# Operand stage of a state-space layer: silu's half folded into weights, its bias as matrix products, evictions and a normalisation on other engines

## The chip, the cores and the metric

The kernel runs on one core of one Trainium2 chip. The metric is the device time of one execution in microseconds. Five engines have instruction queues of their own, each worked through in order: TensorE (PE in the profile; its weight loads are PEld), VectorE (DVE), ScalarE (ACT), GpSimd (POOL), and SyncE (SP), which here only issues transfers. An instruction that waits holds up everything behind it in its own queue, and nothing in the others.

## The reference, cut to what matters

Four residual layers are applied to `x` of 4 images x 128 channels x 64 x 64 pixels, each of the form `x = x + layer(group_norm(x))`: self-attention over the 4096 pixels, a 5x5 convolution, a selective state-space scan in both directions, and a 3x3 convolution. The change lies in the third layer's inputs:

```python
t = einsum('oc,bchw->bohw', Wx, x) + bx          # x is the group-normed image
xc = sum(conv_w[:, k] * up[:, :, k:k+L] for k in range(4))   # causal, 4 taps over t
xc = silu(xc + conv_b)
delta = softplus(xt @ Wd + bd)                   # xt is xc transposed
Bm = xt @ WB
Cm = xt @ WC
# scan: h = exp(delta * A) * h + (delta * xt) * Bm ; y = sum over states of h * Cm + D * xt
```

The two directions have weights of their own for 64 channels each, so that they fill the 128 partitions together. silu is made from a tanh: `silu(p) = (tanh(p/2) + 1) * p/2`.

## The kernel before, in words

The last layer needs nothing from other images, so the images are pipelined. A generator `images()` produces the work of all images in order: attention, the 5x5 convolution (`conv_pairs`), then `scan_prep` and `scan_operands`, which make the scan's operands and store them in DRAM. A second generator, `scan_core`, produces the scan: 256 ticks per image. The main loop writes the program out by hand: after each half tick it takes as much of `images()` as a credit allows (`PACE` 2.8 units per tick, 1.5 for the last image), and each piece of work yields its cost in these units. So attention and convolution of image b+1 stand beside the scan of image b, and the order of every engine's queue is fixed when the program is built. Waits come from the data and from the buffers.

**A tick** of the scan (128 rows x 1024 positions) is: `drive`, a product db on GpSimd (L1027); `decay`, two exponentials da on ScalarE (L1020); `recur`, two scans on VectorE (L1037), which are either followed by two products with the row of C on VectorE (L1040), or by one on GpSimd (`weigh`, L1058); and `collect`, products y on TensorE (L1072) that sum over states. The rows of B and C are read back from DRAM. ScalarE keeps the last column of each scan (L1053).

**The operand stage** (`scan_operands`) works on eight pieces of 512 positions, in slots of an explicit schedule. A slot costs 0.7 units, and a new piece begins every five slots. The steps of piece i, with the slot after its start:

- slots 0 and 1: `taps`, 16 instructions on TensorE (L832): four taps, two directions in two column halves, two instructions each, into the single PSUM bank pt (tag `s`). For the first piece products with `edge` (L838) correct the border.
- slot 4: `halves` on ScalarE: L846 writes (pt + bias)/2 to xc in SBUF, L851 writes tanh((pt + bias)/2), for images 1 to 3 in place over pt, for image 0 to a buffer `w` in SBUF.
- slot 5: `silu` on VectorE (L855): (th + 1) * xc into xc. Only then is the bank pt free for the next taps (for image 0 after L851).
- slots 8, 9 and 12: products with the block-diagonal weights `bdiag` on TensorE (L864), m=0 for delta, m=1 for B, m=2 for C. The products for B and C share one bank (tag `a`).
- slots 11 and 13: `row` on ScalarE (L869) copies B (m=1) and C (m=2) from PSUM to a buffer `w` of four, which SyncE stores.
- slots 10, 12 and 13: `softplus` (L877, L878), `exp` (L904, L909) on ScalarE, `digits` on VectorE (L883, L884).
- after half of the pieces `logs` (L913) on ScalarE, then `join` (L889) and `drives` (L894) on GpSimd.

In one slot, what belongs to an earlier piece stands ahead of what belongs to a later one, and `digits` ahead of `row` for C.

Interleaved with the slots of image b is the start of image b+1: its load, its statistics on VectorE (L378), its group norm, four pieces of `normalise` on ScalarE in place (L369, 1024 columns each), and eight products `keys` pv on TensorE (L396) with copies by ScalarE (L401). After these, attention begins with the scores sc (L464).

Of the kernel before, what the change touches and what calls it, by code (L numbers as in the profile page):

```python
# [24 lines left out]
F32 = mybir.dt.float32  # L25
I32 = mybir.dt.int32
AF = mybir.ActivationFunctionType
ALU = mybir.AluOpType
# [4 lines left out]
P = 128  # L33
# [3 lines left out]
MM = 512  # L37
HALF = P // 2
# [10 lines left out]
BQ, BK, BX, BP, CONVB, BD, DSKIP, MAINB, CONVW, ALOG = 0, 1, 2, 3, 4, 5, 6, 7, 8, 12  # L49
# [3 lines left out]
def conv_preact_kernel(  # L53
# [16 lines left out]
    nc = tc.nc  # L70
# [12 lines left out]
    scale = float(C) ** -0.5  # L83
# [3 lines left out]
    const = ctx.enter_context(tc.tile_pool(name="const", bufs=1))  # L87
# [3 lines left out]
    pools, ready = {}, set()  # L91

    def bank(tag, name):
        return pools.get(tag, ps).tile([P, MM], F32, tag=tag, name=name)
# [20 lines left out]
    ident = const.tile([P, P], F32, name="ident")  # L115
# [11 lines left out]
    def col(i):  # L127
        return vec[:, i : i + 1]


    ssm_sb = early.tile([P, 3, HALF], F32, name="ssm_sb")
    nc.scalar.dma_start(ssm_sb, ssm)
    bdiag = const.tile([P, 3, C], F32, name="bdiag")
    nc.gpsimd.memset(bdiag, 0.0)
    for d in range(2):
        r = slice(d * HALF, (d + 1) * HALF)
        nc.gpsimd.tensor_copy(bdiag[r, :, r], ssm_sb[r, :, :])


    NK, NQ = P // SG, NST // NI  # L140
# [10 lines left out]
    skip = const.tile([P, P], F32, name="skip")  # L151
# [25 lines left out]
    wtap = const.tile([P, KC, C], F32, name="wtap")  # L177
    edge = const.tile([P, KC - 1], F32, name="edge")
    cbias = small.tile([P, 1], F32, tag="cbias", bufs=1, name="cbias")
    hbias = const.tile([P, 1], F32, name="hbias")  # L180

    def scan_constants():

        for k in range(KC):
            ptap = bank("z", f"ptap{k}")[:, :C]
            nc.tensor.matmul(
                ptap, col(CONVW + k).to_broadcast([P, P]), ident, start=True, stop=True
            )
            yield HOP
            nc.vector.tensor_tensor(wtap[:, k, :], wm[:, 3, :], ptap, ALU.mult)  # L190
        for t in range(KC - 1):

            nc.vector.tensor_reduce(
                edge[:, t : t + 1], vec[:, CONVW : CONVW + KC - 1 - t], AX.X, ALU.add
            )
        nc.vector.tensor_tensor(cbias, edge[:, 0:1], col(CONVW + KC - 1), ALU.add)
        nc.vector.scalar_tensor_tensor(cbias, cbias, col(BX), col(CONVB), ALU.mult, ALU.add)
        nc.vector.tensor_scalar(edge, edge, col(BX), -1.0, ALU.mult, ALU.mult)
        nc.vector.tensor_scalar(hbias, cbias, 0.5, None, ALU.mult)
        yield HOP  # L200
        mine = early.tile([P, NI], F32, name="mine")
        nc.vector.tensor_reduce(
            mine, ident.rearrange("p (s i) -> p i s", i=NI), AX.X, ALU.add
        )
        rates = every.rearrange("p k q i -> p (k q) i")
        mine = mine.unsqueeze(1).to_broadcast([P, NK * NQ, NI])
        nc.vector.tensor_tensor(rates, rates, mine, ALU.mult)
        nc.vector.tensor_reduce(a_neg, rates, AX.X, ALU.add)
        yield HOP
        nc.scalar.activation(a_neg, a_neg, AF.Exp)  # L210
        nc.vector.tensor_reduce(
            sel, ident.rearrange("p (s i) -> p s i", i=NI), AX.X, ALU.add
        )
        nc.vector.tensor_scalar(skip, ident, col(DSKIP), None, ALU.mult)
        yield HOP
        nc.vector.tensor_scalar(a_neg, a_neg, -1.0, None, ALU.mult)
        yield HOP
# [66 lines left out]
    def large(n, name):  # L284
        return pools["big"].tile([P, ASIZE], F32, tag=f"A{n % 2}", name=name)
# [6 lines left out]
    def stats_tile(name):  # L292
        return small.tile([P, NM, 6], F32, tag=f"gn_st{name[0]}", name=f"st_{name}")
# [74 lines left out]
    def normalise(dst, src, gn):  # L368
        nc.scalar.activation(dst, src, AF.Identity, scale=gn[0], bias=gn[1])  # L369
# [4 lines left out]
    def attention_start(b, xn):  # L374

        st = stats_tile(f"a{b}")
        for i in range(NM):
            nc.vector.bn_stats(st[:, i, :], xn[:, bass.ts(i, MM)])  # L378
            yield 0.0
        gn = yield from group_norm(st, f"a{b}")  # L380
        while b > 0 and (b - 1, "taps") not in ready:
            yield 0.0
        v = pools["big"].tile([P, VSIZE], F32, tag="V", name=f"v_{b}")
        v = v[:, : NJT * C].rearrange("p (j c) -> p j c", c=C)
        pvs = {}

        def piece(i):
            cut = bass.ts(i, L // 4)
            normalise(xn[:, cut], xn[:, cut], gn)

        def keys(i):

            tag = "s" if b > 0 else "saz"[i % 3]
            pvs[i] = bank(tag, f"pv_{b}_{i}").rearrange("p (t c) -> p t c", c=C)
            for t in range(TPM):
                nc.tensor.matmul(  # L396
                    pvs[i][:, t, :], xn[:, bass.ts(i * TPM + t, P)], wv, start=True, stop=True
                )

        def take(i):  # L400
            nc.scalar.copy(v[:, i * TPM : (i + 1) * TPM, :], pvs.pop(i))  # L401

        piece(0)
        yield SLOT
        for i in range(NM):
            if i % 2 == 0 and i // 2 + 1 < 4:
                piece(i // 2 + 1)
            keys(i)
            yield SLOT
            if b > 0:  # L410
                take(i)
                yield 0.0
            elif i > 0:
                take(i - 1)
        if b == 0:
            take(NM - 1)
        return xn, v
# [394 lines left out]
    def scan_operands(b, xn, mats4, piece):  # L812
# [5 lines left out]
        xc = large(b, f"xc_{b}")[:, :L]  # L818
        delta = pools["big"].tile([P, L], F32, tag="xt", name=f"delta_{b}")
        pts, ths, pzs, pbs, us = {}, {}, {}, {}, {}  # L820

        def taps(i, *ks):
# [4 lines left out]
            for k in ks:  # L827
                lo = L + 2 * pad - 1 - k - t - (MM - 1)
                views = (xn[:, t + k : t + k + MM], xn[:, lo : lo + MM][:, ::-1])
                for d, view in enumerate(views):  # L830
# [6 lines left out]
                    if i == 0 and k == 0:  # L837
# [2 lines left out]
                            tile_position=(0, d * HALF), skip_group_check=True,  # L840
                        )

        def halves(i):

            pt = pts.pop(i)
            nc.scalar.activation(xc[:, bass.ts(i, MM)], pt, AF.Identity, scale=0.5, bias=hbias)  # L846

            ths[i] = pt if b > 0 else pools["bg"].tile(
                [P, MM], F32, tag="w", bufs=4, name=f"th_{b}_{i}"
            )  # L850
            nc.scalar.activation(ths[i], pt, AF.Tanh, scale=0.5, bias=hbias)  # L851

        def silu(i):
            cut = bass.ts(i, MM)
            nc.vector.scalar_tensor_tensor(  # L855
                xc[:, cut], ths.pop(i), 1.0, xc[:, cut], ALU.add, ALU.mult
            )
            if i % 2:
                c = i // 2
                nc.sync.dma_start(xcd[c], xc[:, bass.ts(c, CH)])  # L860
# [5 lines left out]

        def row(i, m):
            bs = pools["bg"].tile([P, MM], F32, tag="w", bufs=4, name=f"bs{m}_{b}_{i}")
            nc.scalar.copy(bs, pbs.pop((i, m)))  # L869
            c, h = divmod(i, CH // MM)  # L870
            nc.sync.dma_start(bc[m - 1][c][:, bass.ts(h, MM)], bs)

# [271 lines left out]
    def program(safe):  # L1144
# [99 lines left out]
        def images():  # L1244
            begun = yield from start(0)
            for b in range(B):
                begun = yield from front(b, *begun)
            for a in range(B - 1):
                yield from stage(a, range(NM), "scan")
                yield from end(a, range(NM))  # L1250
                yield from back(a)
            for pieces, done in ((inner, "inner"), (last, "last")):
                yield from stage(B - 1, pieces, done)
                yield from end(B - 1, pieces)
            yield from stage(B - 1, range(PER), "lower")
            ready.add((B - 1, "staged"))

        with ExitStack() as es, tc.manual_schedule():
# [18 lines left out]
            work = images()  # L1277
# [26 lines left out]
            def result():  # L1304

                while (B - 1, "staged") not in ready:
                    next(work)
                return ends[B - 1][2]

            credit = 0.0  # L1310
            for i in scan_core(mats4, ynds, before, widen, result):
                if i % TICKS == 6 and i > TICKS:
                    ready.add((i // TICKS - 1, "scan"))
                if i == B * TICKS - TICKS // NCH + 6:
                    ready.update({(B - 1, "inner"), (B - 1, "lower")})
                if i == B * TICKS - TICKS // NCH // 2 + 6:
                    ready.add((B - 1, "last"))
                credit = min(credit + pace / 2, pace)
                while credit > 0:
                    credit -= next(work, pace)  # L1320
# [81 lines left out]
```

## Time and profile before

The median of three runs is 4534.42 us (4531.9 to 4534.6); the profiled execution took 4538.3 us.

| stretch (us) | what runs | busiest engine |
|---|---|---|
| 0 to 510 | attention of image 0 alone | PE 99% |
| 510 to 655 | convolution of image 0 alone | PE 92% |
| 655 to 750 | operands of image 0, start of image 1 | none is full |
| 750 to 1600, 1720 to 2550, 2690 to 3525 | attention and convolution of images 1, 2, 3 beside scans 0, 1, 2 | PE 99% |
| 1600 to 1715, 2560 to 2680, 3525 to 3625 | operands of images 1, 2, 3 | none is full |
| 3625 to 4450 | scan 3 beside the last convolutions of images 0 to 2 | DVE 95%, POOL 95% |
| 4450 to 4538 | last convolution of image 3 | PE |

The instructions concerned, from the groups kept apart by shape:

| line | engine | what | count | mean ns |
|---|---|---|---|---|
| L832 | PE | taps, 64 columns of weights x 512 | 512 | 663 |
| L846 | ACT | half of pt to xc | 32 | 688 |
| L851 | ACT | tanh | 32 | 660 in PSUM, 689 to SBUF |
| L855 | DVE | silu | 32 | 685, 779 for image 0 |
| L869 | ACT | rows of B and C | 64 | 595 |
| L369 | ACT | normalise the next image, 1024 columns | 16 | 1245 |
| L1027 | POOL | db, two inputs, 1024 columns | 1024 | 2366 |
| L515 | POOL | copy, 512 columns | 8 | 663 |

A mean is the time from an instruction's start to its end. On an engine in sequence they overlap a little: L851 starts some 0.57 us after L846. Two tap instructions run beside each other, one in each column half.

### The profile page before, as it was taken

What the parts mean: (1) busy time and instruction counts of PE and PEld (TensorE: products, weight loads), DVE (VectorE), ACT (ScalarE), POOL (GpSimd) and SP (SyncE); (2) the same over time, 40 slices, a digit from 0 to 9 for tenths busy, and PEclk for the clock granted to TensorE, in tenths of its full rate; (3) what the DMA queues carried; (4) which work ended last, traced back from release to release, by engine and by line L of the source; (5) the groups of instructions that cost most, each with busy time, mean ns of one, the idle gap of its engine ahead of it and who ended that gap; (6) DMA issues with size and microseconds to landing.
All of it is one profiled execution on the core that took longest, in us unless ns stands there. A gap on an engine that the chain in (4) does not pass through costs nothing. (4 is left out here: it accounts for less than half of the span.)

```text
span 4538.3 us, 43660 instructions
## 1 busy us (share of the span) xinstructions
PE 4022.5 (89%) x13568; PEld 1492.3 (33%) x13568; DVE 3649.1 (80%) x3619; ACT 2400.1 (53%) x4420; POOL 3636.2 (80%) x1730
## 2 busy tenths in 40 slices
PE   8999998999999979999999879999999658576767
PEld 4444433333333323333333223333333112121212
DVE  4722106999998978999989879999999699999993
ACT  3333217666665466666654566666654654544441
POOL 3433207999998969999989889999999799999992
PEclk9999999999999989999999989999999878687878
DMA  1000006445544555544545555545445566656561
GB/s 62 6 1 1 5 29 239 175 170 174 175 174 155 181 202 201 175 174 169 179 154 181 185 207 180 169 170 175 175 159 178 211 235 204 231 188 230 186 232 47
DMA packets 210579, 719.48 MB, mean 159 GB/s; under 512 B 24864, under 2 KB 25760, under 8 KB 210208
## 3 DMA queue, kind: packets, MB, share of 16 engines
q1 hardware_dynamic: 208736, 715.87, 44.8%
q8 instruction: 109, 1.79, 0.2%
q14 instruction: 134, 1.10, 0.1%
q10 hardware_dynamic: 1600, 0.73, 0.1%
HBM read 649.07 MB, written 67.44 MB: 158 GB/s over the span
## 5 line engine op out<-in xcount | busy, mean ns | idle before, releaser
L1027 POOL TENSOR_TENSOR db<-dx,br 128x1024 f32<-128x1024 f32 x1024 | 2399.7, 2366 | 234.0 <-DMA dx<-dxd 59.7
L1020 ACT ACTIVATE da<-de,a_neg 128x512 f32<-128x512 f32 (+1 forms) x1795 | 1342.2, 751 | 745.4 <-DVE da L1037 451.2
L464 PE MATMUL sc<-r,x 128*128 128x512 f32 x2048 | 1082.4, 611 | 18.2 <-ACT r L433 12.4
L476 PE MATMUL acc<-pt,v 128*128 128x512 f32 x2048 | 1046.6, 593 | 1.6
L1058 POOL TENSOR_TENSOR hc<-hc,cr 128x1024 f32<-128x1024 f32 x406 | 959.7, 2364 | 14.3 <-ACT last L1053 11.7
L470 ACT ACTIVATE pt<-sc 128x512 f32<-128x512 f32 x1024 | 604.3, 590 | 563.9 <-PE sc L464 555.2
L1072 PE MATMUL y<-hc,sel 128*32 128x512 f32 x4096 | 656.9, 651 | 271.5 <-POOL hc L1058 267.0
L1040 DVE TENSOR_TENSOR hc<-da,cr 128x512 f32<-128x512 f32 (+1 forms) x1067 | 828.4, 776 | 68.9 <-issue 1.8
L1037 DVE TENSOR_TENSOR_SCAN da<-da,last,db 128x512 f32<-128x512 f32 (+1 forms) x464 | 728.2, 1569 | 27.3 <-POOL db L1027 21.7
L1037 DVE TENSOR_TENSOR_SCAN da<-da,da,db 128x512 f32<-128x512 f32 x449 | 577.9, 1287 | 13.6 <-ACT da L1020 12.7
L464 PEld LDWEIGHTS sc<-r,x 128*128 128x128 f32 x2048 | 359.1, 190 | 605.0 <-issue 374.3
L476 PEld LDWEIGHTS acc<-pt,v 128*128 128x128 f32 x2048 | 387.5, 190 | 497.2 <-issue 477.9
L1037 DVE TENSOR_TENSOR_SCAN hc<-da,hc,db 128x512 f32<-128x512 f32 x322 | 413.1, 1283 | 61.2 <-ACT da L1020 30.4
L1037 DVE TENSOR_TENSOR_SCAN hc<-da,last,db 128x512 f32<-128x512 f32 (+1 forms) x304 | 455.9, 1500 | 6.6 <-ACT da L1020 2.4
L518 POOL TENSOR_TENSOR sidep<-sidep,pt 128x512 f32<-128x512 f32 x120 | 170.4, 1420 | 280.0 <-ACT pt L470 277.9
L1072 PEld LDWEIGHTS y<-hc,sel 128*32 128x32 f32 x4096 | 94.7, 111 | 728.5 <-POOL hc L1058 359.5
L643 PE MATMUL pcm<-xpm,cw 128*128 128x512 f32 x576 | 290.5, 652 | 30.5 <-ACT xpm L369 30.5
L760 PE MATMUL pe<-df,cw 128*128 128x512 f32 x640 | 289.5, 598 | 0.0
L518 DVE TENSOR_TENSOR sided<-sided,pt 128x512 f32<-128x512 f32 x120 | 97.2, 810 | 231.0 <-ACT pt L470 229.7
L1037 DVE TENSOR_TENSOR_SCAN da<-da,db 128x512 f32<-128x512 f32 (+1 forms) x154 | 231.2, 1501 | 32.5 <-POOL db L1027 16.4
L498 PE MATMUL zp<-pt,ones 128*32 128x512 f32 x1536 | 204.8, 595 | 5.0 <-DVE xs L562 5.0
L1053 ACT COPY last<-da 128x1 f32<-128x1 f32 x469 | 73.0, 156 | 246.9 <-DVE hc L1040 245.1
(196 smaller groups left out, 2719.5 us busy)
## 6 DMA issues: line engine op xcount, KB each, us to landing
br<-bm SPq DMA_DIRECT2D x512, 512.0 KB, 5.2
cr<-cm SPq DMA_DIRECT2D x512, 512.0 KB, 3.9
de<-dd SPq DMA_DIRECT2D x64, 512.0 KB, 4.6
dx<-dxd SPq DMA_DIRECT2D x64, 512.0 KB, 6.5
x<-in_x_dram SPq DMA_DIRECT2D x16, 512.0 KB, 5.1
xs<-in_x_dram SPq DMA_DIRECT2D x16, 512.0 KB, 5.6
xsd<-xs SPq DMA_DIRECT2D x16, 512.0 KB, 5.1
xcd<-xc SPq DMA_DIRECT2D x16, 512.0 KB, 2.8
```

Source lines behind the costliest of these rows:

```text
L464: nc.tensor.matmul(sc, xn[:, bass.ts(j, P)], rq[blk], start=True, stop=True)
L470: nc.scalar.activation(pt, sc, AF.Exp)
L476: nc.tensor.matmul(acc[blk], v[:, j, :], ring[:, u % NRING, :], start=j == 0, stop=j == NJT - 1)
L518: eng.tensor_tensor(s, s, ring[:, u % NRING, :], ALU.add)
L643: nc.tensor.matmul(acc.rearrange("p (r w) -> p r w", w=W), weights[:, t, :], xp[:, y : y + RPM, dx : dx + W], start=t == 0, stop=t == k * ...
L760: nc.tensor.matmul(flat(acc), cw[:, w * K5 + dx, :], view(r, dx), start=k == 1, stop=k == total and (n == 0 or not lean),)
L1020: nc.scalar.activation(da, rep["de", b, c, d, g][:, bass.ts(h, size)], AF.Exp, scale=a_neg[:, at(i)])
L1027: nc.gpsimd.tensor_tensor(dbs[i], rep["dx", b, c, d, g], rows["b", b, c, d, q], ALU.mult)
L1037: nc.vector.tensor_tensor_scan(h, da, db[:, cut], before, ALU.mult, ALU.add)
L1040: nc.vector.tensor_tensor(hc[:, cut], h, rows["c", b, c, d, q][:, cut], ALU.mult)
L1058: nc.gpsimd.tensor_tensor(hcs[i], hcs[i], rows["c", b, c, d, q], ALU.mult)
L1072: nc.tensor.matmul(y[r : r + SG, :], sel, hcs[i - KG + 1 + gg][:, bass.ts(h, MM)], start=q == 0, stop=False, tile_position=(0, r), skip_gr ...
```

## The change

It has four parts, which share one aim: fewer instructions on ScalarE in the operand stage.

1. The half of silu moves into the weights. `silu` now makes (tanh(p/2) + 1) * p, twice the value, and `bdiag` carries 0.5 for delta, 0.25 for B and 0.5 for C, `skip` carries 0.5. (The drive is delta * xc * B, so that B's row takes the second half.) The instruction L846 and `hbias` go.
2. The bias enters pt on TensorE, after the second tap, as an identity product with `cbias` repeated over 512 columns: one matrix product for each direction and piece, in the taps' form. `silu` reads pt from PSUM, and tanh goes to a buffer `w` in SBUF for all images.
3. For images 1 to 3 the rows of C (m=2) are copied from PSUM by VectorE. Rows of B, and both rows of image 0, stay on ScalarE.
4. For images 1 to 3 the first normalisation (`piece` in `attention_start`) is done by GpSimd, in place, with a multiply and an add of two columns.

A default in a `next` call in `result` changes nothing as long as work is left.

```diff
+        for m, factor in enumerate((0.5, 0.25, 0.5)):
+            nc.gpsimd.tensor_scalar(bdiag[r, m, r], ssm_sb[r, m, :], factor, None, ALU.mult)
-        nc.gpsimd.tensor_copy(bdiag[r, :, r], ssm_sb[r, :, :])
...
-        nc.vector.tensor_scalar(hbias, cbias, 0.5, None, ALU.mult)
...
-        nc.vector.tensor_scalar(skip, ident, col(DSKIP), None, ALU.mult)
+        nc.vector.tensor_scalar(skip, ident, col(DSKIP), 0.5, ALU.mult, ALU.mult)
...
         def piece(i):
             cut = bass.ts(i, L // 4)
-            normalise(xn[:, cut], xn[:, cut], gn)
+            if b > 0:
+                nc.gpsimd.tensor_scalar(xn[:, cut], xn[:, cut], *gn, ALU.mult, ALU.add)
+            else:
+                normalise(xn[:, cut], xn[:, cut], gn)
...
+                if k == 1:
+                    for d in range(2):
+                        r = slice(d * HALF, (d + 1) * HALF)
+                        nc.tensor.matmul(
+                            pt[r, :], ident[:, r], cbias.to_broadcast([P, MM]),
+                            start=False, stop=False,
+                            tile_position=(0, d * HALF), skip_group_check=True,
+                        )
...
         def halves(i):
-            pt = pts.pop(i)
-            nc.scalar.activation(xc[:, bass.ts(i, MM)], pt, AF.Identity, scale=0.5, bias=hbias)
-            ths[i] = pt if b > 0 else pools["bg"].tile(
-                [P, MM], F32, tag="w", bufs=4, name=f"th_{b}_{i}"
-            )
-            nc.scalar.activation(ths[i], pt, AF.Tanh, scale=0.5, bias=hbias)
+            ths[i] = pools["bg"].tile([P, MM], F32, tag="w", bufs=4, name=f"th_{b}_{i}")
+            nc.scalar.activation(ths[i], pts[i], AF.Tanh, scale=0.5)
...
         def silu(i):
             cut = bass.ts(i, MM)
             nc.vector.scalar_tensor_tensor(
-                xc[:, cut], ths.pop(i), 1.0, xc[:, cut], ALU.add, ALU.mult
+                xc[:, cut], ths.pop(i), 1.0, pts.pop(i), ALU.add, ALU.mult
             )
...
         def row(i, m):
-            nc.scalar.copy(bs, pbs.pop((i, m)))
+            (nc.scalar.copy if m == 1 or b == 0 else nc.vector.tensor_copy)(bs, pbs.pop((i, m)))
```

More of the change, by code (lines that the diff above doesn't have):

```diff
@@ L179, in conv_preact_kernel @@
     cbias = small.tile([P, 1], F32, tag="cbias", bufs=1, name="cbias")
-    hbias = const.tile([P, 1], F32, name="hbias")
     def scan_constants():
@@ L1306, in result @@
                 while (B - 1, "staged") not in ready:
-                    next(work)
+                    next(work, None)
                 return ends[B - 1][2]
```

## The prediction

> **What bounds the kernel now.** I read the page's busy shares and its 40 slices first, then the windows by 100 us, then the timeline of each engine in one stretch where every engine dips.
>
> ```profile
> PE 4022.5 (89%) x13568; PEld 1492.3 (33%) x13568; DVE 3649.1 (80%) x3619; ACT 2400.1 (53%) x4420; POOL 3636.2 (80%) x1730
> ...
> PE   8999998999999979999999879999999658576767
> ...
> DVE  4722106999998978999989879999999699999993
> ```
>
> Slices 7 to 30 hold three nearly equal cycles (attention, 5x5 convolution and operands of the next image beside the scan of the last), slices 32 to 39 the last scan. The windows show what the cycle consists of (columns: PE, PEld, DVE, ACT, POOL busy of 100 us, PE clock, DMA share, GB/s):
>
> ```profile
> 1600.00:1700.00 100.00, 75.96 (x288) 27.82 (x288) 71.91 (x91) 72.44 (x115) 64.60 (x33) 0.88 0.61 216
> ...
> 1900.00:2000.00 100.00, 99.72 (x377) 36.20 (x375) 95.65 (x99) 64.34 (x132) 94.73 (x42) 1.00 0.50 176
> ...
> 2600.00:2700.00 100.00, 70.21 (x257) 26.33 (x259) 72.19 (x80) 66.97 (x115) 77.02 (x39) 0.81 0.60 216
> ```
>
> Outside the operand stage TensorE is at 99%, so a delay of TensorE there is never made up. In the operand stage (1600 to 1700, 2560 to 2680, 3525 to 3625; for image 0 at 660 to 750) no engine is full: it runs on a chain between engines. All of the change but its set-up lies in these four stages. One piece of the chain, on TensorE, ScalarE and VectorE:
>
> ```profile
> 1629.78 3.66 PE L832 MATMUL pt<-xn,wtap 128*64 128x512 f32 x16 [1.33 <-DVE xc L855]
> 1633.36 2.93 PE L864 MATMUL pb<-xc,bdiag 128*128 128x512 f32 x6
> 1637.64 3.66 PE L832 MATMUL pt<-xn,wtap 128*64 128x512 f32 x16 [1.35 <-DVE xc L855]
> ```
>
> ```profile
> 1634.53 0.59 ACT L869 COPY bs<-pb 128x512 f32<-128x512 f32 x1 [3.04 <-PE pb L864]
> ...
> 1635.63 0.68 ACT L846 ACTIVATE xc<-pt,hbias 128x512 f32<-128x512 f32 x1
> 1636.20 0.66 ACT L851 ACTIVATE pt<-pt,hbias 128x512 f32<-128x512 f32 x1
> ```
>
> ```profile
> 1632.26 0.69 DVE L884 TENSOR_TENSOR delta<-delta,pb 128x512 f32<-128x512 f32 x1
> 1632.86 1.28 DVE L1037 TENSOR_TENSOR_SCAN hc<-da,last,db 128x512 f32<-128x512 f32 x1
> 1634.17 1.28 DVE L1037 TENSOR_TENSOR_SCAN hc<-da,hc,db 128x512 f32<-128x512 f32 x1
> 1636.90 0.69 DVE L855 SCALAR_TENSOR_TENSOR xc<-pt,xc 128x512 f32<-128x512 f32 x1 [1.44 <-ACT pt L851]
> ```
>
> Taps end at 1633.4; ScalarE waits for product m=2, copies it, then makes the two halves; VectorE finishes silu at 1637.6 and frees the one bank of pt; the next taps start. TensorE fills all but 1.35 us of that 4.2 us with products. So TensorE is already near its limit here: 3.43 us of taps plus 2.93 of products, plus 1.06 when a collect falls in, in a period of about 8. VectorE meanwhile does a tick's scans under the taps.
>
> **What the Trainium skill says.** "TensorE: Matmul & The Clock Gate", Part 3 (packing small matmuls): matmuls on different column tiles run concurrently. The trace agrees: 16 tap instructions of some 590 ns each fit into 3.66 us. Part 1 of that page: an idle array falls to half clock until it has been busy for some 3.4 us; here the first taps (1603.4, after 7.03 us idle) and the last (1669.4, 6.02 us in place of 3.66, after 6.69 idle) run so. "GPSIMD Engine Reference", section 4.1: a one-input operation is roughly at line rate on GpSimd, a two-input one about twice as slow. The trace agrees for the copy (663 ns for 512 columns, against 2366 ns for a two-input 1024). "VectorE: DVE Perf Modes", "Why PSUM operands drop a tier": an fp32 copy out of PSUM runs at one element a cycle; the trace has only small ones (155 ns for 4 columns, 283 ns for 128).
>
> **The change, part by part.**
>
> Bias products: two halves of two instructions per piece, in the taps' form. 16 tap instructions take 3.43 us apart from the tail, so 4 take 0.86; at half clock 1.7. With 32 pieces that is 27.5 us at full clock, in a stage where TensorE has about 1.35 us of slack per piece at most. A moving operand that repeats one column isn't in the trace: I price it as a tap.
>
> Identity half removed: 0.57 us (the start-to-start step of L846 to L851) less between taps and silu; silu reads pt from PSUM as it did (L855, 0.69). For image 0 the old th lay in SBUF and pt was free after Tanh; now it is held until silu, 0.7 us later. The 0.5 in weights and skip costs set-up only, beside attention.
>
> Rows of C: the copy on VectorE is bounded by L163's slope, (283-155)/124 = 1.03 ns per column: 0.68 us; the ScalarE copy (0.59) is the other end. 24 x 0.68 = 16 us of VectorE, which alone would hide. What matters is the wait: in the changed program's order the copy stands behind the two `digits` instructions and AHEAD of the tick's scans. It waits for product m=2, which TensorE makes only after the piece's taps. So VectorE's scans, which ran under the taps, now run after them, and silu behind them. From the built order, a tick stands between copy and silu in 11 of the 18 pieces concerned (pieces 2 to 7 of images 1 to 3): in 4 with two scans and two multiplies (2 x 1.28 + 2 x 0.69 = 3.95 us), in 7 with two scans (2.56). Then from the end of the taps: 1.12 (product) + 0.68 + 2.56 + 0.69 + 0.15 of signals = 5.2 us, or 6.6 with multiplies, in place of 4.2. Without a tick it is 2.6, less than TensorE's own 2.93 of products, and the old 1.35 wait is gone.
>
> Normalising by GpSimd: 12 instructions of 1024 columns. Lower end 1.2 us (the copy row at about 1 ns per column), upper end 2.37 (the two-input row); I take 1.3, as one tensor is read. ScalarE loses 12 x 1.15 us where it has no gaps (9.83 and 9.94 us of 10 in 1680 to 1700). GpSimd gains 5.2 us per image where, from 1708 on, it has no gaps either; behind each piece are products db and hc of the scan, and the key products pv wait for the piece.
>
> Sum, for an image 1 to 3 up to its last taps: bias 7 x 0.86 plus half-clock 0.5 = +6.5; ticks behind the copy: (7 x 1.0 + 4 x 2.4) / 3 = +5.5; pieces without a tick (7 of 18): 2.3 x -1.2 = -2.8; Identity in the first two pieces -1.2. Net +8. From the last taps to the next scores: bias at half clock +1.3, ScalarE relieved by 4 x 1.15 and two copies, -5.6, of which GpSimd's new pieces take back about half, +2.5. Net -2. So +6 for images 1 and 2. Image 3 has no next image and only part of the relief: +7. Image 0: period 6.56 (taps at 701.25 and 707.80) becomes 4.3 of taps, 2.93 of products and about 0.35 of steps and wait for silu, 7.6: six such periods, +6; relief and GpSimd as above, -1: +5. Together 5 + 6 + 6 + 7 = +24, so 4534.4 + 24 = 4558 us. After each stage TensorE, and in the tail VectorE and GpSimd, are full, so I count nothing as absorbed.
>
> **The rivals.**
>
> ScalarE is the true pacer, so the change is faster. For: it stalls on products (3.04 us above) and is full near the end of each stage, where VectorE waits for its decays. If bias products hid in the old waits (0.86 against 1.35: -0.5 x 24 = -12) and the relief of 5.6 were kept whole in three stages (-17): 4534 - 29 = 4505. Against: TensorE's queue leaves no room for the bias where a collect falls in, and VectorE's order.
>
> A wash: the head-of-line wait is half of what I think, because the products of m=2 come early or scans are late anyway, and the relief is kept: 24 - 11 - 8 = +5, 4539. It counts as no change.
>
> GpSimd becomes the bound: pieces at 2.37 us (+1.1 x 12 = 13), and TensorE waits on hc after each stage because GpSimd lags more than TensorE does (some 3 us in three stages, 9): 4580. For: GpSimd is at 10.00 of 10 in every window from 1710 to 1760. Against: over the whole cycle it has 6% free.
>
> **How the numbers follow.** Forecast 0.45, GpSimd as bound 0.16, wash 0.13, ScalarE as pacer 0.26. Slower therefore 0.61, same 0.13, faster 0.26. The range reaches to 4510, a little short of the whole of the fast rival, and to 4595, past the GpSimd one with copies and bias at their upper ends.
>
> **What would show it.** Taps to taps should be 9 to 11 us where a tick stands behind the copy and 7.5 to 8.5 where none does; bias products 0.86 us per piece; idle time of VectorE's L878 copy put down to TensorE's products; in TensorE's idle before taps, silu with 2 to 4 us in place of 1.35. Wrong would be: periods under 7.9 us throughout, or a first score of image 2 earlier than 1714 us less what image 0 gained.

## The result, and the profile after

| | before | after |
|---|---|---|
| median of four runs, us | 4533.97 (4531.9 to 4534.6) | 4565.95 (4562.33 to 4569.77) |
| span of the profiled execution, us | 4538.3 | 4568.0 |

The ratio of the times is 1.0071, with a 95% interval of 1.0059 to 1.0083: the change makes the kernel 32 us slower. The forecast was 24 us slower.

The page of the changed kernel, busy shares and slices:

```profile
PE 4056.2 (89%) x13696; PEld 1504.3 (33%) x13696; DVE 3662.4 (80%) x3642; ACT 2356.2 (52%) x4352; POOL 3649.4 (80%) x1746
...
PE   8999998999999979999999879999999658585767
...
DVE  4722106999998978999999779999999799999993
```

ScalarE does 44 us less, TensorE 34 us more, VectorE and GpSimd 13 us more each. No share moves by more than a point, so the page cannot tell why the kernel is slower. The same windows as before the change (columns: length, then busy time and count of PE, PEld, DVE, ACT, POOL, then PE clock, DMA share, GB/s):

```profile
1600.00:1700.00 100.00, 75.93 (x297) 27.04 (x298) 72.64 (x103) 55.86 (x90) 62.33 (x37) 0.90 0.59 210
1900.00:2000.00 100.00, 99.52 (x384) 36.04 (x381) 94.83 (x99) 64.67 (x134) 91.77 (x40) 1.00 0.49 171
2600.00:2700.00 100.00, 70.35 (x264) 26.50 (x261) 69.02 (x81) 53.98 (x91) 69.60 (x39) 0.85 0.54 188
```

The aim was reached: ScalarE's 72.4 and 67.0 us of the two operand windows are now 55.9 and 54.0. Outside, TensorE is at 99.5% as it was. Four groups of the changed kernel (busy us, mean ns, then the idle time ahead of them and what ended it):

```profile
L851 PE MATMUL pt<-cbias,ident 128*64 128x512 f32 x128 | 39.5, 647 | 0.0
L878 DVE COPY bs<-pb 128x512 f32<-128x512 f32 x24 | 16.5, 689 | 40.6 <-PE pb L873 40.6
L391 POOL TENSOR_SCALAR x<-x,rs_a,nb_a 128x1024 f32<-128x1024 f32 x12 | 14.4, 1201 | 0.0
L860 ACT ACTIVATE th<-pt 128x512 f32<-128x512 f32 x32 | 19.1, 597 | 68.0 <-PE pt L836 68.0
```

The first gives the bias products, in the taps' form and at their price. The second is the one to read: VectorE stood 40.6 us before its 24 copies, always for TensorE's products. The last says that ahead of its 32 tanh ScalarE stood 68.0 us, by the trace always for the taps and never for a free buffer `w`, of which tanh now takes one for every image. One piece of image 1 shows how it hangs together. TensorE:

```profile
1635.43 3.21 PE L836 MATMUL pt<-xn,wtap 128*64 128x512 f32 x8 [2.42 <-DVE xc L864]
1638.36 1.56 PE L851 MATMUL pt<-cbias,ident 128*64 128x512 f32 x4
1639.72 1.92 PE L836 MATMUL pt<-xn,wtap 128*64 128x512 f32 x8
1641.57 3.03 PE L873 MATMUL pb<-xc,bdiag 128*128 128x512 f32 x6
1646.66 1.94 PE L836 MATMUL pt<-xn,wtap 128*64 128x512 f32 x8 [2.05 <-DVE xc L864]
1648.40 1.06 PE L851 MATMUL pt<-cbias,ident 128*64 128x512 f32 x4
1649.26 1.91 PE L836 MATMUL pt<-xn,wtap 128*64 128x512 f32 x8
1651.10 1.12 PE L873 MATMUL pb<-xc,bdiag 128*128 128x512 f32 x2
```

VectorE in the same piece:

```profile
1636.66 0.69 DVE L893 TENSOR_TENSOR delta<-delta,pb 128x512 f32<-128x512 f32 x1
1642.73 0.69 DVE L878 COPY bs<-pb 128x512 f32<-128x512 f32 x1 [5.38 <-PE pb L873]
1643.34 1.27 DVE L1046 TENSOR_TENSOR_SCAN hc<-da,last,db 128x512 f32<-128x512 f32 x1
1644.65 1.28 DVE L1046 TENSOR_TENSOR_SCAN hc<-da,hc,db 128x512 f32<-128x512 f32 x1
1645.85 0.66 DVE L864 SCALAR_TENSOR_TENSOR xc<-th,pt 128x512 f32<-128x512 f32 x1
```

VectorE has nothing to do from 1637.4 to 1642.7, since the copy at the head of its queue waits for a product that TensorE makes only after the taps. The two scans, whose operands were ready at 1636.5, come after it, silu after them, and TensorE, with all its products done at 1644.6, waits 2.05 us for silu. Before the change VectorE did these scans without waiting for the product. The lines in the prediction put them at 1632.86 to 1635.45, so they ran mostly after the taps' end at 1633.4, beside TensorE's products and ScalarE's copy and halves, and not "under the taps" as the prediction reads them. The bias products show as the step from 1648.40 to 1649.26.

A second cost shows in the same lines. The taps and bias products from 1635.43, after a wait of 2.42 us, took 6.2 us, those from 1646.66, after 2.05 us, 4.5. The granted clock was 0.59 from 1635.43 to 1638.40 and 1.00 from 1646.66 to 1649.20.

Where the 29.7 us between the two profiled executions lie. A stage is counted from the first taps to the first exponential of the next image's scores (for image 3 to the first product po of the last convolution); a cycle is what lies between stages:

| us | image 0 | cycle | image 1 | cycle | image 2 | cycle | image 3 | rest |
|---|---|---|---|---|---|---|---|---|
| before | 93.8 | 849.4 | 112.1 | 847.9 | 119.2 | 843.1 | 141.9 | 870.7 |
| after | 98.5 | 851.0 | 115.1 | 848.1 | 125.5 | 849.1 | 148.8 | 872.2 |
| difference | +4.8 | +1.6 | +3.0 | +0.2 | +6.3 | +6.0 | +6.9 | +1.6 |

The start up to image 0's first taps differs by -0.7. So 21 us came in the four stages, 9 outside.

### The profile page after: what moved, and what is told of

Same layout as the page of the kernel before. It is cut to its first block, busy times and chain, and to the rows that moved or that the text cites. A ratio compares the mean times of both kernels' runs of the same rounds, so it can differ in the third digit from the quotient of the medians.

```text
span 4568.0 us, 43896 instructions
## 1 busy us (share of the span) xinstructions
PE 4056.2 (89%) x13696; PEld 1504.3 (33%) x13696; DVE 3662.4 (80%) x3642; ACT 2356.2 (52%) x4352; POOL 3649.4 (80%) x1746
## 5 line engine op out<-in xcount | busy, mean ns | idle before, releaser
L1049 DVE TENSOR_TENSOR hc<-da,cr 128x512 f32<-128x512 f32 (+1 forms) x1067 | 828.4, 776 | 69.5 <-PE acc L480 1.3
L1046 DVE TENSOR_TENSOR_SCAN da<-da,da,db 128x512 f32<-128x512 f32 x449 | 577.9, 1287 | 13.1 <-ACT da L1029 12.5
L1046 DVE TENSOR_TENSOR_SCAN hc<-da,hc,db 128x512 f32<-128x512 f32 x322 | 413.1, 1283 | 47.7 <-ACT da L1029 15.1
L836 PE MATMUL pt<-xn,wtap 128*64 128x512 f32 x512 | 143.5, 655 | 69.5 <-DVE xc L864 35.2
```

The source lines that it names most:

```text
L1046: nc.vector.tensor_tensor_scan(h, da, db[:, cut], before, ALU.mult, ALU.add)
L1049: nc.vector.tensor_tensor(hc[:, cut], h, rows["c", b, c, d, q][:, cut], ALU.mult)
```

## The experiments

Times are medians; the difference is to the runs of the kernel before beside them, the interval that of the ratio. "Stages" is the sum of the four stages in the trace, 467.0 us for the kernel before; "taps" is from the start of the first taps to the start of the last for images 0, 1, 2, 3, before the change 47.6, 66.1, 68.2, 58.7 us.

| run | us | difference | ratio, 95% | stages | taps of images 0 to 3 |
|---|---|---|---|---|---|
| after | 4565.95 | +32.0 | 1.0059 to 1.0083 | 488.0 | 52.6, 69.8, 75.7, 64.8 |
| parts 1, 2 alone | 4545.75 | +12.5 | 1.0017 to 1.0039 | 476.5 | 52.6, 66.5, 69.2, 60.1 |
| part 3 alone | 4540.28 | +7.1 | 1.0006 to 1.0022 | 467.0 | 47.5, 68.2, 70.9, 63.2 |
| part 4 alone | 4531.49 | -1.7 | 0.9987 to 1.0004 | 460.0 | 47.5, 62.8, 68.4, 59.1 |
| after without part 3 | 4547.04 | +13.8 | 1.0018 to 1.0038 | 473.3 | 52.8, 66.7, 70.4, 59.0 |
| after without bias products | 4542.99 | +10.1 | 1.0014 to 1.0036 | 469.9 | 48.3, 67.4, 70.6, 60.0 |
| after without part 4 | 4557.46 | +24.5 | 1.0041 to 1.0068 | 488.2 | 52.7, 69.8, 74.6, 67.4 |
| after, copy behind silu | 4563.86 | +30.9 | 1.0052 to 1.0079 | 489.8 | 64.8, 71.8, 73.3, 62.4 |
| parts 3, 4, copy behind silu | 4538.51 | +5.6 | 1.0004 to 1.0017 | 474.1 | 55.5, 71.5, 70.1, 62.1 |
| after, copy behind silu for images 1 to 3 | 4549.87 | +15.0 | 1.0024 to 1.0051 | 474.8 | 52.5, 69.4, 73.4, 62.9 |
| after, join and drives on VectorE | 4566.40 | +31.6 | 1.0058 to 1.0086 | 495.9 | 52.6, 70.5, 74.8, 69.5 |
| part 4, join and drives on VectorE | 4535.74 | +0.9 | 0.9992 to 1.0009 | 464.1 | 47.7, 63.5, 66.3, 63.1 |
| order for images 1 to 3, no bias | 4531.65 | -3.5 | 0.9985 to 1.0002 | 456.9 | 49.0, 67.0, 69.3, 58.9 |

A trace is one execution, and executions of one kernel differ (part 3 alone took 4532.5 to 4547.1 us). The traced one of the kernel before took 4540.1 us, 6 above its median; those of part 3 alone and part 4 alone took 4534.2 and 4527.8, 6 and 4 below theirs. So two sums of stages can differ by several us without any edit.

The next table splits the stretches from first to last taps of images 1 to 3 into the time in which TensorE was busy and the time in which it was idle (sums of three stretches, us):

| run | length | TensorE busy | TensorE idle |
|---|---|---|---|
| before | 193.0 | 150.3 | 42.8 |
| parts 1, 2 alone | 195.8 | 165.2 | 30.6 |
| part 3 alone | 202.3 | 158.3 | 44.0 |
| after without part 3 | 196.2 | 165.5 | 30.6 |
| after | 210.2 | 170.3 | 39.9 |
| after, copy behind silu for images 1 to 3 | 205.7 | 167.5 | 38.2 |

The theory at the start was that of the prediction: bias products on TensorE's path, and scans behind a waiting copy. The rivals were ScalarE as the pacer, and GpSimd as the bound.

**Parts 1 and 2 alone.**

```diff
-            (nc.scalar.copy if m == 1 or b == 0 else nc.vector.tensor_copy)(bs, pbs.pop((i, m)))
+            nc.scalar.copy(bs, pbs.pop((i, m)))
...
-            if b > 0:
-                nc.gpsimd.tensor_scalar(xn[:, cut], xn[:, cut], *gn, ALU.mult, ALU.add)
-            else:
-                normalise(xn[:, cut], xn[:, cut], gn)
+            normalise(xn[:, cut], xn[:, cut], gn)
```

(These lines are against the changed kernel.)

> The kernel before with parts 1 and 2 alone: the half in the weights, the bias as identity products; rows of C and the normalisation stay on ScalarE. My theory (the bias products are work on TensorE's path): 32 pieces at 0.86 us and some at half clock, less the Identity half in the pieces that wait for it, +17 to +25 us over the kernel before. Rival (ScalarE paces the stage, the bias hides in TensorE's old waits of 1.35 us): -10 to 0 us. If the cost of the whole change sits in the other two parts: 0 to +5 us.

+12.5 us: between the theories. Image 0's taps take 5.0 us more, near the 6 worked out. In images 1 to 3 they take only 0.5, 0.9 and 1.4 us more, not 6.5. TensorE in this run:

```profile
1632.16 1.94 PE L833 MATMUL pt<-xn,wtap 128*64 128x512 f32 x8 [0.46 <-DVE xc L861]
1633.93 1.03 PE L848 MATMUL pt<-cbias,ident 128*64 128x512 f32 x4
1634.79 1.89 PE L833 MATMUL pt<-xn,wtap 128*64 128x512 f32 x8
1636.61 2.93 PE L870 MATMUL pb<-xc,bdiag 128*128 128x512 f32 x6
1640.24 1.94 PE L833 MATMUL pt<-xn,wtap 128*64 128x512 f32 x8 [0.71 <-DVE xc L861]
```

The piece takes 8.08 us (1632.16 to 1640.24) with the bias and took 7.86 before (1629.78 to 1637.64). The bias did not hide: the loop runs taps, product m=2, ScalarE's copy, tanh, silu, taps, and the bias adds 0.86 us to it. But the Identity half, 0.57 us, stood on the same loop and is gone, and TensorE's wait for silu fell from 1.35 to 0.71. The sum is 0.86 - 0.57 = +0.29 us per piece (an estimate), seven times, +2 per image, somewhat more than the table has. The split says the same: TensorE is busy for 15.0 us longer and idle for 12.2 us less, which is 0.58 us for each of 21 pieces.

**Part 3 alone, and the change without part 3.** The edit of the first is this line in the kernel before; the second puts the old line into the changed kernel.

```diff
-            nc.scalar.copy(bs, pbs.pop((i, m)))
+            (nc.scalar.copy if m == 1 or b == 0 else nc.vector.tensor_copy)(bs, pbs.pop((i, m)))
```

> The kernel before with part 3 alone: rows of C of images 1 to 3 copied by VectorE. My theory (the copy waits for the products of m=2 ahead of the tick's scans, so that scans run after the taps and silu after them): +4 to +14 us, and silu later after the taps where a tick stands between. Rival (16 us of copies hide on VectorE, ScalarE is relieved): -8 to 0 us.

> The changed kernel with rows of C back on ScalarE (parts 1, 2 and 4 stay). My theory: 4 to 14 us below the changed kernel's 4566, so +18 to +28 us over the kernel before; taps-to-taps of pieces with a tick fall by 1 to 2.4 us. Rival (the copies relieve ScalarE and cost nothing): at or above 4566, +32 us or more over the kernel before.

Part 3 alone costs 7.1 us, as the head-of-line wait has it. Taken out of the changed kernel it returns 18, beyond the upper end of that theory and far from the rival's. The two pieces per image in which a tick makes the loop longer take 10.0 to 11.2 us in place of 7.9 to 8.8 with part 3 alone; together with the bias 10.9 to 12.0. Without part 3 they fall back to 8.1 to 8.8, by 2.1 to 3.4 us.

The difference between the two prices fits what the run before showed: once the copy of C is on VectorE, the loop is taps, product, copy, scans, silu. It no longer passes ScalarE, so the removed Identity half pays for nothing there, and the bias stands on the loop in full. The split supports it: without part 3, TensorE's idle time is 30.6 us, and with it 39.9, so that 9 of the 12 us that parts 1 and 2 had won are gone. Alone, part 3 adds only 1.2 us of idle time, as shorter waits in other pieces make up for the longer ones. But from first to last taps part 3 costs 9 us alone and 14 in company, so 5 of the 11 us between the two prices are accounted for; the rest lies elsewhere and stays open.

What part 3 adds alone from first to last taps is mostly, 8.0 of 9.3 us, TensorE taking longer for the same instructions (182 per image). Image 1 of this run:

```profile
1624.06 5.35 PE L832 MATMUL pt<-xn,wtap 128*64 128x512 f32 x16 [2.42 <-DVE xc L855]
1634.43 5.35 PE L832 MATMUL pt<-xn,wtap 128*64 128x512 f32 x16 [2.05 <-DVE xc L855]
1643.68 3.66 PE L832 MATMUL pt<-xn,wtap 128*64 128x512 f32 x16
```

The granted clock was 0.55 from 1624.06 to 1627.50 and 0.54 from 1634.43 to 1637.50. So a wait of TensorE can cost more than its own length. It doesn't always: taps at full speed follow a wait of 2.05 us in the changed kernel (1646.66), and slow ones, 5.35 us, follow one of 2.06 us in the kernel before (1612.75). How much of the 7.1 us is this varies from execution to execution.

**Part 4 alone.**

```diff
-            normalise(xn[:, cut], xn[:, cut], gn)
+            if b > 0:
+                nc.gpsimd.tensor_scalar(xn[:, cut], xn[:, cut], *gn, ALU.mult, ALU.add)
+            else:
+                normalise(xn[:, cut], xn[:, cut], gn)
```

> The kernel before with part 4 alone: the first normalisation of images 1 to 3 on GpSimd. My theory (ScalarE is relieved of 12 x 1.15 us where it is full, GpSimd gives back half as its queue lags behind TensorE): -8 to 0 us. Rival (GpSimd becomes the bound: scores wait for its drives, products db and hc come later for the whole cycle): +6 to +15 us.

-1.7 us, no difference that these runs can tell. In the trace the stages are 7 us shorter, but that is the fastest of 13 executions and 12.3 us shorter as a whole than the trace of the kernel before, so it does not show how much of the relief of ScalarE is kept. What the start of attention then waits for (ScalarE, first exponential of image 2's scores, of this run):

```profile
1705.10 0.68 ACT L1023 ACTIVATE da<-de,a_neg 128x512 f32<-128x512 f32 x1
1710.03 0.60 ACT L473 ACTIVATE pt<-sc 128x512 f32<-128x512 f32 x1 [4.25 <-POOL xc L897]
```

The exponentials go into a buffer that `delta` held, so they wait until GpSimd has read `delta` in its last `drives`. In the kernel before this wait was 1.39 us:

```profile
1715.53 0.60 ACT L470 ACTIVATE pt<-sc 128x512 f32<-128x512 f32 x1 [1.39 <-POOL xc L894]
```

**The change without the bias products.** The block under `if k == 1` goes.

> The changed kernel without the four bias products of a piece (the bias is left out; with these inputs it is zero). After the first four runs the cost of bias and rows together is more than that of each alone. Theory: where the copy of C closes a loop of taps, product, copy, scans and silu, the bias lies on that loop in full; so the pieces with a tick fall by 0.86 us from some 11 to some 10.1 us, image 0's from 7.5 to 6.6, and the kernel is 10 to 18 us below the changed one (+14 to +22 us over the kernel before). Rival (the bias hides, and the extra cost is the ring of four w buffers that tanh now shares with the rows, or GpSimd): only image 0's 5 us are saved, 4 to 7 us below the changed kernel.

22 us below the changed kernel by the differences (10.1 against 32.0), more than the theory's upper end and far from the rival's. Image 0's taps give 4.3 us back, images 1 to 3 give 2.4, 5.1 and 4.7; four of the six tick pieces fall by the 0.86 us of the bias, as from 10.90 to 10.04. The stages together are 18.1 us shorter; the rest lies outside them. `w` buffers and GpSimd are here as in the changed kernel, so they are not what these 22 us are lost to.

**The change without part 4.** The old line of `piece` in the changed kernel.

> The changed kernel with the normalisation back on ScalarE (parts 1 to 3 stay). Theory (part 4 brings a little, as it did alone): 0 to 7 us above the changed kernel, +32 to +39 us over the kernel before. Rival (GpSimd's lag is what makes the parts cost more together than alone): 5 to 14 us below the changed kernel, +18 to +27 us over the kernel before.

7.5 us below the changed kernel by the differences (24.5 against 32.0), where the theory had it above; that is in the rival's range, but the intervals of the two ratios overlap. So part 4 brings nothing here, and probably costs. The stages are the same (488.2 and 488.0), so what it costs lies in the cycles between them. GpSimd holds the start of attention back for longer. First exponential of image 2's scores, changed kernel:

```profile
1719.77 0.68 ACT L1029 ACTIVATE da<-de,a_neg 128x512 f32<-128x512 f32 x1
1724.20 0.60 ACT L474 ACTIVATE pt<-sc 128x512 f32<-128x512 f32 x1 [3.74 <-POOL xc L903]
```

Without part 4:

```profile
1717.21 0.68 ACT L1026 ACTIVATE da<-de,a_neg 128x512 f32<-128x512 f32 x1
1719.73 0.60 ACT L471 ACTIVATE pt<-sc 128x512 f32<-128x512 f32 x1 [1.84 <-POOL xc L900]
```

The last taps of image 1 began at 1678.8 and 1676.1, so from there it takes 45.4 us with part 4 and 43.6 without.

**Another order: the copy right behind silu.** The copy of C moves behind silu of the piece after next, and the product of m=1 and the next taps stand behind it.

```diff
-            at(t, taps, i, 0, 1)
-            at(t + 1, taps, i, 2, 3)
...
-            at(t + 9, row_product, i, 1)
...
-            at(t + 13, row, i, 2)
+        for i in range(NM):
+            at(EVERY * i + 15, row, i, 2)
+            at(EVERY * i + 10, row_product, i, 1)
+        for i in range(NM):
+            at(EVERY * i, taps, i, 0, 1)
+            at(EVERY * i + 1, taps, i, 2, 3)
```

> The changed kernel with another order alone: the copy of C stands right behind the silu of the piece after next on VectorE, and the product of m=1 and the next taps behind it. The copy still waits for the product of m=2, but no scan stands between that wait and silu. Theory (head-of-line wait): pieces with a tick fall from 11 to 8 to 8.7 us, 12 to 24 us below the changed kernel, +8 to +20 us over the kernel before. Rival (VectorE's added work or the w buffers, not the order): within 5 us of the changed kernel.

By its total a miss for the theory, 2 us below the changed kernel (1 by the differences), in the rival's range. The trace says why: image 0, where the copies are still ScalarE's, pays 12.2 us more for this order (64.8 against 52.6), while the other three stages are 11 us shorter. In image 0 the products now wait 1.84 us for a copy on ScalarE (at 683.34 and 694.36), and the taps of three pieces took 6.2 us in place of 4.5. The same order on the kernel before with parts 3 and 4:

> The kernel before with parts 3 and 4 and the order of the run above, no bias products, half and bias on ScalarE as before. Theory: without the wait for ScalarE's copy a piece needs some 6.6 to 7.5 us in place of 7.6 to 8.8, which makes 15 pieces some 1.2 us shorter, and part 4 brings its 2: 8 to 24 us below the kernel before. Rival (the stage is held by something else, such as products of delta and the softplus chain): within 5 us of the kernel before.

+5.6 us, a miss for the theory; the rival's 5 lies inside the interval. Image 0 again takes 8 us more (55.5 against 47.5). So the order was tried for images 1 to 3 alone, with the old slots under `if b == 0` (the run before, in its expectation, is the changed kernel in this order for all images):

> The order of the run before (the copy of C right behind silu, product m=1 and the next taps behind it) for images 1 to 3 alone; image 0 keeps the changed kernel's order. In the run before, image 0's first to last taps went from 52.7 to 64.8 us and hid what images 1 to 3 gained. Theory (head-of-line wait): image 0 back at 52.7, so 10 to 18 us below the changed kernel, +14 to +22 us over the kernel before. Rival (the order brings nothing): within 4 us of the changed kernel.

17 us below the changed kernel by the differences, in the theory's range. With no edit but the order, half of the loss is gone. In the traces 4.5 us of it lie between first and last taps, 8.3 between the last taps and the end of the stages, the rest outside; the theory's pieces are the first of these alone, and why the others fell is not followed here. VectorE of this run, then TensorE:

```profile
1638.03 0.66 DVE L864 SCALAR_TENSOR_TENSOR xc<-th,pt 128x512 f32<-128x512 f32 x1
1638.61 0.68 DVE L878 COPY bs<-pb 128x512 f32<-128x512 f32 x1
1639.21 1.27 DVE L1055 TENSOR_TENSOR_SCAN hc<-da,last,db 128x512 f32<-128x512 f32 x1
1640.58 1.28 DVE L1055 TENSOR_TENSOR_SCAN hc<-da,hc,db 128x512 f32<-128x512 f32 x1
```

```profile
1639.34 1.12 PE L873 MATMUL pb<-xc,bdiag 128*128 128x512 f32 x2 [1.26 <-DVE bs L878]
1640.40 1.94 PE L836 MATMUL pt<-xn,wtap 128*64 128x512 f32 x8
```

The copy no longer waits, and the scans run beside the product of B and the taps that start at 1640.40. Most pieces with a tick now take 8.4 to 8.8 us, but one per image still 10.1 to 10.5.

**Join and drives on VectorE.** To test GpSimd's lag by itself, in the changed kernel and in the kernel before with part 4:

```diff
-                nc.gpsimd.tensor_tensor(delta[:, cut], delta[:, cut], us.pop(i), ALU.add)
+                (nc.vector if b > 0 else nc.gpsimd).tensor_tensor(delta[:, cut], delta[:, cut], us.pop(i), ALU.add)
...
-            nc.gpsimd.tensor_tensor(xc[:, cut], delta[:, cut], xc[:, cut], ALU.mult)
+            (nc.vector if b > 0 else nc.gpsimd).tensor_tensor(xc[:, cut], delta[:, cut], xc[:, cut], ALU.mult)
```

> The changed kernel with the sums and products of join and drives on VectorE for images 1 to 3, in place of GpSimd. Theory (after the operands of images 1 and 2 the first exponential of the scores waits for GpSimd's drives, 3.74 and 3.82 us, because normalise, join and drives stand in GpSimd's queue with db and hc): that wait goes and GpSimd's lag with it, 5 to 14 us below the changed kernel. Rival (GpSimd's lag holds nothing up, or VectorE pays as much for 16 added instructions per image): within 4 us of the changed kernel or above it.

> The kernel before with part 4 and with join and drives on VectorE for images 1 to 3. With part 4 alone the first exponential of image 2's scores waited 4.25 us for GpSimd's drives. Theory: that wait goes in two images, 5 to 14 us below the kernel before. Rival: within 4 us of it.

No difference in either, so the rival of these two runs holds. In the first of them the wait on GpSimd is gone, yet the first exponential of image 2's scores comes at 1724.15, no earlier than the 1724.20 of the changed kernel. VectorE's four sums from 1705.09 took 9.49 us, and ScalarE waited behind them for a scan. One line of ScalarE and two groups of VectorE:

```profile
1715.75 0.69 ACT L1029 ACTIVATE da<-de,a_neg 128x512 f32<-128x512 f32 x1 [7.28 <-DVE hc L1046]
```

```profile
L898 DVE TENSOR_TENSOR delta<-delta,u 128x512 f32<-128x512 f32 x24 | 30.4, 1316 | 6.0 <-ACT u L922 6.0
L903 DVE TENSOR_TENSOR xc<-delta,xc 128x1024 f32<-128x1024 f32 x12 | 22.2, 1877 | 0.0
```

The following cycle is 7 us shorter than the changed kernel's (840.8 against 848.1 us), and image 3's stage 11 us longer (160.0 against 148.8). What was won in one place was lost in another.

**The floor.** The order for images 1 to 3, without the bias products.

> The run with the copy behind silu for images 1 to 3, without the bias products (the bias is left out; it is zero with these inputs). It is the floor for any cheaper way to add the bias. Theory (wait order and bias are the two costs, and in this order the bias hides in part): 8 to 18 us below that run, so -3 to +7 us over the kernel before: what is left of the change brings nothing. Rival (the relief of ScalarE is worth something once both costs are gone): 10 us or more below the kernel before.

18 us below the run with the bias and 3.5 below the kernel before, with an interval that holds 1: the theory's numbers, just past their edges. Without these two the kernel is back where it was, so order and bias are the two costs. Even a bias that costs nothing would leave a kernel that cannot be told from the one before. No version with the bias in it that was run beats the kernel before by more than its interval.

## Why the forecast was right, and where it was off

- **All happens in four stages, and nothing is made up elsewhere.** The stages gave +4.8, +3.0, +6.3 and +6.9 us, 21 together, where the steps had +5, +6, +6 and +7. So their sum came out as worked out, though in part by luck, as the next point shows. The step that was off is the last of the sum, which counted what lies outside the stages as zero: it is 9 us, six of them in the third cycle. About half of the six can be named. TensorE waited 3.1 us in that cycle for GpSimd's hc, where it had not waited for it before, and its products right after the longer wait were slow (2.08 us for two, 1.12 a little later):

```profile
2707.03 1.28 PE L1081 MATMUL y<-hc,sel 128*32 128x512 f32 x6 [2.21 <-POOL hc L1067]
2708.24 2.08 PE L468 MATMUL sc<-r,x 128*128 128x512 f32 x2
```

In the other two cycles these waits did not grow (5.0 against 5.4 us, 0.6 against 1.6). The rest stays open: the third cycle took 842 to 848 us in the other runs, and single executions of the changed kernel differ by 7 us.
- **Up to the last taps +8, from there -2.** Measured for images 1 to 3: +3.7, +7.5 and +6.0 up to the last taps, and -0.7, -1.2 and +0.9 from there. Less loss and less relief than worked out, which offset each other: here luck helped the sum. Slow taps, which the forecast counted with 0.5 us up to the last taps, were more: in four of the six tick pieces the taps took 5.7 or 6.2 us in place of 4.5.
- **Bias products at 0.86 us.** The size was right (1648.40 to 1649.26), and taken out of the whole change they return 22 us, near the 27.5 of the bare sum. Alone, parts 1 and 2 cost 12.5. The step gave the Identity half back in two pieces only. That fits the whole change, where VectorE copies C; the first run shows that it counts in every piece as long as ScalarE does.
- **Scans behind the copy.** Right in mechanism, and in the size of the wait per piece; a tick stands behind the copy in 11 of 18 pieces, as worked out. From the end of the taps to the next taps the forecast was 5.2 us with a two-scan tick; 1641.57 to 1646.66 is 5.1. With multiplies it was 6.6; in image 2 it is 6.45 (2602.10 to 2608.55). Net it was +2.7 per image, 8 in all, and part 3 alone cost 7.1. In company it cost 18, of which the Identity half's lost saving is a part. The forecast priced the parts beside each other, as they stand in the whole change. The expectations of the single parts carried these prices over and did not see that one part changes the price of the other: 17 to 25 us was expected of parts 1 and 2, 12.5 came.
- **Normalise on GpSimd at 1.3 us.** It takes 1.20, some 1.2 ns per column, in agreement with "GPSIMD Engine Reference", section 4.1, in the Trainium skill: a one-input operation runs roughly at line rate. The product with two inputs takes 2.3 ns per column. The relief of 5.6 less 2.5 us per image was too much: part 4 brings 1.7 us in all alone, and nothing in company. The mis-sized term is what GpSimd takes back, counted as half.
- **Rivals.** ScalarE as the pacer is half true: with its copy on the loop, the removed Identity half pays for two thirds of the bias. But relieving it of copies and normalisations brought no time. GpSimd as the bound was seen in waits of 3.74 and 4.25 us at the start of attention and in TensorE's waits for hc in one cycle; moving its work to VectorE did not shorten the kernel, and its pieces took 1.20 us, not 2.37. The wash is out.

## What to carry to other kernels

Before an eviction is moved to an engine that looks idle, look at what it will wait for and what is queued behind it there: 16 us of copies fit into VectorE's gaps, and the kernel still lost 7 us by them alone and 18 beside the bias, with scans standing behind the wait. A wait that it causes on TensorE can cost more than its length, as the taps after two such waits ran at about half the clock. An instruction saved counts only on the loop that paces the stage, and a second edit can move that loop to another engine, so parts that cost 12.5, 7.1 and -1.7 us alone cost 32 together. If such a copy must move, its place in the queue comes first: here the order alone was worth 17 us.

## What the hardware showed that was not expected

Two-input VectorE instructions with all operands in SBUF were stretched beside GpSimd's (the run with join and drives on VectorE in the changed kernel). The sums of L898, 512 columns, took 0.675 us at the shortest and 2.83 at the longest, the products of L903, 1024 columns, 1.20 to 3.38. Meanwhile GpSimd's products took 2.78 to 3.33 in place of 2.35 us. All stretched sums and products stood beside a GpSimd instruction; the twelve sums and seven products that stood beside none took 0.69 and 1.22 us at most. "SBUF — State Buffer", "Who interferes with whom", in the Trainium skill says that a VectorE instruction with two SBUF inputs contends with a GpSimd instruction that reads SBUF; 2.83 us for a sum, as long as the GpSimd product beside it, agrees. That in a row of such instructions both sides are stretched is what these runs add. VectorE's products of the scan (L1049 in this run), whose first input `da` lies in PSUM, ran beside GpSimd's at their 0.69 us for 512 columns.

A moving operand that repeats one column costs what a full one does: 647 ns for L851, 655 ns for the taps.
